# Attention over an adjacency matrix: which steps are summed through A (E - 1) g

## The chip, the cores and the metric

One core of one Trainium2 chip. The metric is the device time of one execution in microseconds (us); lower is better. The kernel before was run three times.

## The reference

Two layers on x (4096 x 512) with a 0/1 matrix adj (4096 x 4096). Layer 0 is graph attention with 8 heads of 64 features:

```python
feats = jnp.einsum('nf,hfo->hno', X, W)
dense = s_self[:, :, None] + s_neigh[:, None, :]
dense = jnp.where(dense > 0, dense, ALPHA * dense)
dense = dense * A[None, :, :]
attn = jax.nn.softmax(dense, axis=-1)
out = jnp.einsum('hij,hjo->hio', attn, feats) + b[:, None, :]
```

The result goes through relu, is added to x and normalised (layernorm). The softmax runs over all 4096 columns: a place where A is 0 has score 0 and so weight 1. Layer 1 is attention inside 32 graphs of 128 rows each, with adj added to the scores twice, again with a residual and a layernorm.

## The kernel before, in words

exp(leaky_relu(s_i + s_j)) is, up to factors of i alone and j alone, a maximum of a value of i and a value of j. So for a head and a node j, the weights against 1024 rows i are `max(p_row, d) * a`, one VectorE instruction on a 128 x 1024 tile: 128 partitions hold nodes j, the free dimension holds rows i, a is the transposed piece of the adjacency matrix. The text calls this product q.

Work is cut into passes r = 0 to 3 (a pair of heads each), chunks c = 0 to 3 (1024 rows) and steps j = 0 to 31 (128 nodes). Three sums are built in PSUM for every chunk, over its 32 steps:

- `acc` gets q times the features g_s (L1581): 8 matmul instructions a step, shown as 16 rows, each on a quarter of TensorE's columns;
- `accf` gets a times the features f_s (L1558): 4 matmuls a step, 128 x 128 weights and 512 columns;
- `dens` gets the marks times e_b (L1597), where a mark says whether q is above a bound. ScalarE makes most marks (L1544), VectorE every eighth (L1539).

At the end of a chunk `sums_to_rows` adds them up: L1278 reads accf into ys, L1286 adds acc, ScalarE copies dens (L1288), and later pieces turn ys back to rows (L1335, L1338, L1361, L1362). accf, acc and dens have one buffer each.

A *folded* step leaves its four L1558 matmuls out. VectorE makes q in two instructions for each head instead of one: L1522, `max(p_row, d) * U_row`, and L1525, `(q - c) * a`. The product of this q with g_s goes into accf (L1581, "accf<-q" in the profile), and its marks come from L1529. `folded(j)` (L1447) says which steps these are; only the first and the last pass have any. U_row is a pair of rows of the current chunk, 512 KB each, loaded by SP in `rows_for_folded` (L1453): in tiles "ck" in the first pass, "hst" and "U_row" in the last. SP, too, loads a (L635, "at"), f_s, g_s, p_row and u_row.

The first three passes go in cycles of 8 steps, the last in groups of 4. In a cycle TensorE does first all L1558, then all L1581, then dens. q has 6 buffers in the last pass and 8 in the first. In the first pass the kernel also turns the matrix: a_b pieces are loaded by POOL (L605), transposed on TensorE (L617), cast on ScalarE (L628) and written to HBM by POOL (L629) for the later passes.

In the last pass, layer 1 runs between the sums. PLANS (L1396) gives, for each group of a chunk, the pieces of the two blocks "a" and "b" that TensorE does between L1558 and L1581. Group 7 has "aaba": `rows_out` of rows 0 and 1 (L1200, read by L1202 on VectorE), `values` of 2 and 3 (L1186, read by L1194), the scores of block b (L1141, read by L1150), `rows_out` of 2 and 3. These pieces share three PSUM banks. The order on TensorE is the order of the program; the instructions of VectorE, ScalarE, POOL and SP are put in order by a scheduler when the kernel is built.

Of the kernel before, what the change touches and what calls it, by code (L numbers as in the profile page):

```python
# [404 lines left out]
def adjacency_streamed_path(  # L405
# [32 lines left out]
    NT = N // P  # L438
# [23 lines left out]
    g_d = dram.tile([PR, NT // 4, P, 4 * FP], F32, name="g_d")  # L462
    f_d = dram.tile([PR, NT // 4, P, 4 * 2 * FP], F32, name="f_d")
    FOLDED = (0, PR - 1)
    FOLDS = {4: (1,), 5: (0, 1), 6: (0, 1, 2)}, {2: (1,), 4: (1,), 5: (0, 1), 6: (0, 1, 2)}
    HU = 2 * len(FOLDED)
    pu_d = dram.tile([2 * H + HU, N], F32, name="pu_d")
    at_d = dram.tile([NCH, NT, P, C], F32, name="at_d")
# [957 lines left out]
    def main_pass(r, ae=None, wide=4):  # L1426

        for c in range(NCH):
# [18 lines left out]
            def folded(j):  # L1447

                if r == PR - 1:
                    return r in FOLDED and c > 0 and j % 4 in FOLDS[c > 1].get(j // 4, ())  # L1450
                return r in FOLDED and j % 8 == 2 and (0 if c else 8) < j < NT - 8

            def rows_for_folded():  # L1453

# [35 lines left out]
            for j0 in range(0, NT, wide):  # L1490
# [16 lines left out]
                if any(map(folded, range(NT))) and j0 == (4 if r else 0):  # L1507
                    rows_for_folded()
# [6 lines left out]
                for j in cycle:  # L1515
                    for h in range(2):
# [3 lines left out]
                        if folded(j):  # L1520
                            cn = c_all[r][:, j, h : h + 1]
                            nc.vector.scalar_tensor_tensor(  # L1522
                                q, p_row[h], d_j, U_row[h], op0=OP.max, op1=OP.mult
                            )
                            nc.vector.scalar_tensor_tensor(  # L1525
                                q, q, cn, ats[r, c, j].bitcast(F32), op0=OP.subtract, op1=OP.mult
                            )
                            mark = marks[j, h] = sgp.tile([P, C], FP8, name="mark")
                            nc.scalar.activation(  # L1529
                                mark, q, AF.Sigmoid, bias=below_0, scale=2.0**80, saturate=False  # L1530
                            )
                            continue
# [22 lines left out]
                for j in cycle:  # L1555
                    for w in range(0 if folded(j) else 2):
                        for s in range(2):
                            nc.tensor.matmul(  # L1558
                                accf[:, s, :],
                                f_s[j // 4][:, j % 4, w, :],  # L1560
                                ats[r, c, j][:, ts(s, HB)],
                                start=(j == 0 and w == 0),
                                stop=(j == NT - 1 and w == 1),
                            )
# [92 lines left out]
@with_exitstack  # L1657
def tile_gat_then_graph_attention(ctx: ExitStack, tc: tile.TileContext, *args: bass.AP):
    nc = tc.nc
    keep = ctx.enter_context(tc.tile_pool(name="flag", bufs=1))  # L1660
    flag = keep.tile([1, 1], I32, name="flag")
    adjacency_streamed_path(tc, flag, *args)
    other = nc.values_load(flag[0:1, 0:1], min_val=0, max_val=1)
    with tc.If(other > 0):
        general_path(tc, *args)
# [42 lines left out]
```

## Time and profile before

| | |
|---|---|
| median of 3 runs | 2040.63 us (2040.04 to 2043.24) |
| profiled execution | 2043.19 us, its span 2041.3 us |
| mean granted TensorE clock | 0.994 |
| TensorE busy | 2005.9 us, 98% |
| VectorE busy | 1744.8 us, 85% |
| ScalarE busy | 1533.1 us, 75% |
| POOL busy | 231.0 us |

The profile comes from one execution. PE is TensorE, DVE VectorE, ACT ScalarE, SP and POOL the engines that issue DMAs. L1558 is line 1558 of the kernel. A group's row gives the line, the engine, the operation, its output and inputs, the shapes and the count, then the busy time and the mean of one in ns, then the idle time of the engine before them and what ended it. A timeline row has the start, the time that it covers and, in brackets, the idle time before it with its releaser. Matmuls overlap at their ends, so a row's duration is a little longer than the distance to the next row's start. Setup takes the first 160 us, the first pass runs to 567, the last from about 1355 to 1920.

### The profile page before, as it was taken

How to read it: one execution, taken by the hardware profiler on the slowest of the kernel's cores; microseconds unless marked ns; L12 is line 12 of the kernel's file. 1: busy time of each engine (PE TensorE's matmuls, PEld its weight loads, DVE VectorE, ACT ScalarE, POOL GpSimd, SP SyncE). 2: the span in 40 equal slices, each digit the busy share in tenths (PEclk: the TensorE clock that was granted, in tenths of full speed). 3: DMA queues.
4: the chain of work that ended last, by engine and by line, in shares of the span. 5: the costliest groups of instructions: out<-in, count | busy, mean ns of one | idle time of the engine just before them, and what ended most of it. 6: DMA issues, size and time to landing. Idle time of an engine off the chain costs nothing.

```text
span 2041.3 us, 38200 instructions
## 1 busy us (share of the span) xinstructions
PE 2005.9 (98%) x14981; PEld 1030.0 (50%) x14981; DVE 1744.8 (85%) x2219; ACT 1533.1 (75%) x1872; POOL 231.0 (11%) x362
## 2 busy tenths in 40 slices
PE   8999999999999999999999999999999999999997
PEld 7885545444444444444444544444444444445443
DVE  5668898898999998798999989999997897889754
ACT  3348988788888889788899889999786566567420
POOL 1222222222200000000000000000020210211111
PEclk9999999999999999999999999999999999999999
DMA  6899999999999999788999999989975775775211
GB/s 206 240 320 280 283 286 288 285 280 282 316 377 342 346 359 342 261 311 292 318 321 338 313 328 338 335 277 368 323 277 186 249 255 173 232 273 176 73 55 44
DMA packets 209386, 558.70 MB, mean 274 GB/s; under 512 B 25052, under 2 KB 66012, under 8 KB 209196
## 3 DMA queue, kind: packets, MB, share of 16 engines
q1 hardware_dynamic: 144844, 433.65, 61.0%
q0 software_dynamic: 62272, 121.98, 23.3%
q8 instruction: 120, 1.97, 0.4%
q10 hardware_dynamic: 2080, 0.52, 0.1%
q14 instruction: 70, 0.57, 0.1%
HBM read 499.13 MB, written 107.28 MB: 297 GB/s over the span
## 4 chain that ended last, share of the span: by engine, by line
PE 85%; DMA 7%; DVE 5%; issue 1%; ACT 1%; SPq 0%; POOL 0%; POOLq 0%; DVEq 0%; ACTq 0%
PE acc L1581 35%; PE accf L1558 20%; PE ps_fe L818 5%; PE ps_m L1186 5%; PE ps_m L1114 5%; PE dens L1597 5%; DMA a_b<-in_adj_dram 4%; DVE q L1534 3%; PE accf L1581 2%; PE ps_m L1141 1%; PE ps_m L1200 1%; DMA hp_l<-hs_d 1%; PE ps_m L617 1%; DMA at_d<-at 1%; PE ps_m L1043 1%
## 5 line engine op out<-in xcount | busy, mean ns | idle before, releaser
L1534 DVE SCALAR_TENSOR_TENSOR q<-p_row,d_all,at 128x1024 f32<-128x1024 f32 x962 | 1168.1, 1279 | 106.0 <-PE acc L1581 78.8
L1544 ACT ACTIVATE mark<-q,nb_all 128x1024 fp8e4<-128x1024 f32 x834 | 926.8, 1144 | 174.7 <-DVE q L1534 160.1
L1581 PE MATMUL acc<-q,g_s 128*32 128x512 f32 x7696 | 853.7, 594 | 1.1 <-DVE q L1534 0.4
L1581 PEld LDWEIGHTS acc<-q,g_s 128*32 128x32 f32 x7696 | 250.2, 110 | 557.2 <-issue 496.3
L1558 PE MATMUL accf<-at,f_s 128*128 128x512 f32 x1924 | 469.3, 400 | 1.7 <-ACT at L628 1.6
L1558 PEld LDWEIGHTS accf<-at,f_s 128*128 128x128 f32 x1924 | 357.2, 189 | 107.3 <-issue 27.8
L1249 ACT ACTIVATE ck<-ck,neg_half_f 128x1024 f32<-128x1024 f32 x128 | 146.0, 1141 | 28.5 <-DMA ck<-in_adj_dram 28.4
L1250 ACT ACTIVATE ck<-ck,neg_quarter 128x1024 f32<-128x1024 f32 x128 | 146.3, 1143 | 1.8
L1597 PE MATMUL dens<-mark,e_b 128*6 128x512 fp8e4 x2048 | 125.3, 379 | 2.5 <-DVE mark L1539 2.5
L818 PE MATMUL ps_fe<-w_sb_f,xT_f 128*128 128x264 f32 (+1 forms) x512 | 121.6, 395 | 1.7 <-ACT xT_f L730 1.7
L628 ACT CAST at<-ps_m 128x1024 fp32r<-128x1024 fp8e4 x124 | 116.3, 1022 | 4.8 <-issue 2.0
L1186 PE MATMUL ps_m<-wvT,x1T 128*128 128x512 f32 x256 | 114.2, 594 | 0.0
L1114 PE MATMUL ps_m<-x1T,M_sb 128*128 128x512 f32 x256 | 113.1, 595 | 0.0
L818 PEld LDWEIGHTS ps_fe<-w_sb_f,xT_f 128*128 128x128 f32 x512 | 100.5, 200 | 16.2 <-ACT xT_f L730 2.3
L1372 POOL DMA_DIRECT2D hs_d<-hst x12 | 10.7, 896 | 828.1 <-DVE hst L1362 817.5
L1539 DVE TENSOR_SCALAR mark<-q,d_all 128x1024 fp8e4<-128x1024 f32 x128 | 96.2, 751 | 4.7
L629 POOL DMA_DIRECT2D at_d<-at x128 | 69.1, 540 | 272.5 <-ACT at L628 94.0
L1597 PEld LDWEIGHTS <-e_b 128*6 128x6 bf16 x2048 | 55.9, 86 | 80.1 <-issue 38.2
L1529 ACT ACTIVATE mark<-q,below 128x1024 fp8e4<-128x1024 f32 x62 | 69.6, 1153 | 24.5 <-DVE q L1525 24.2
L1114 PEld LDWEIGHTS ps_m<-x1T,M_sb 128*128 128x128 f32 x256 | 48.0, 190 | 58.9 <-issue 57.1
L1525 DVE SCALAR_TENSOR_TENSOR q<-q,c_all,at 128x1024 f32<-128x1024 f32 x62 | 77.3, 1273 | 0.0
L1186 PEld LDWEIGHTS ps_m<-wvT,x1T 128*128 128x128 f32 x256 | 47.7, 190 | 56.3 <-issue 55.1
(207 smaller groups left out, 1294.9 us busy)
## 6 DMA issues: line engine op xcount, KB each, us to landing
at<-at_d SPq DMA_DIRECT2D x384, 512.0 KB, 6.1
f_s<-f_d SPq DMA_DIRECT2D x128, 512.0 KB, 7.8
at_d<-at POOLq DMA_DIRECT2D x128, 512.0 KB, 19.1
ck<-in_adj_dram SPq DMA_DIRECT2D x128, 512.0 KB, 5.5
g_s<-g_d SPq DMA_DIRECT2D x128, 256.0 KB, 5.9
f_d<-fst POOLq DMA_DIRECT2D x16, 1024.0 KB, 7.5
a_b<-in_adj_dram POOLq DMA_DIRECT2D x32, 512.0 KB, 21.7
p_row<-pu_d SPq DMA_DIRECT2D x32, 512.0 KB, 6.7
```

The source lines that it names most:

```text
L628: ends_of_setup["ACT"] = nc.scalar.copy(at, both[:, :, k])
L818: nc.tensor.matmul(pf[:, q, :, cols], tile_j(xTs[k][:, c].rearrange("p u n -> p (u n)"), u), w_sb[:, c, 4 * q : 4 * q + 4, cols], start=(c ...
L1114: nc.tensor.matmul(pz, L1["M"][:, f, ts(c, P)], x1T[:, f, :], start=(f == 0), stop=(f == FC - 1),)
L1186: nc.tensor.matmul(pv, x1T[:, f, ts(u, P)], L1["wvT"][:, f, :], start=(f == 0), stop=(f == FC - 1),)
L1249: tc.keep_in_program_order(nc.scalar.activation(ck, ck, AF.Square, bias=neg_half))
L1250: nc.scalar.activation(ck, ck, AF.Abs, bias=neg_quarter, accum_out=binp[:, k : k + 1])
L1534: ends_of_setup["Q"] = nc.vector.scalar_tensor_tensor(q, p_row[h], d_j, ats[r, c, j].bitcast(F32), op0=OP.max, op1=OP.mult)
L1539: nc.vector.tensor_scalar(mark, q, d_j, None, op0=OP.is_gt, saturate=False)
L1544: nc.scalar.activation(mark, q, AF.Sigmoid, bias=nb_all[:, j, hh : hh + 1], scale=BIG, saturate=False,)
L1558: nc.tensor.matmul(accf[:, s, :], f_s[j // 4][:, j % 4, w, :], ats[r, c, j][:, ts(s, HB)], start=(j == 0 and w == 0), stop=(j == NT - 1 an ...
L1581: nc.tensor.matmul(dst[o : o + 32, s, :], g_s[j // 4][:, j % 4, h, o % FH : o % FH + 32], qs[j, h][:, ts(s, HB)], start=(j == 0), stop=(j ...
L1597: nc.tensor.matmul(dens[lo : lo + 6, :], e_b[:, j, 2 * r + h, :], marks[j, h][:, ts(s, HB)], start=(j == 0), stop=(j == NT - 1),)
```

## The change

Other steps are folded. In the first pass: before, j = 10 and 18 in chunk 0, and 2, 10 and 18 in chunks 1 to 3 (11 steps); after, 8, 16 and 24 in each chunk (12 steps). In the last pass, chunk 0 has none; the steps 28 and 29 (group 7) are added in chunks 1 and 2, chunk 3 stays as it is (20 steps before, 24 after). In all 31 steps before and 36 after.

```diff
-    FOLDS = {4: (1,), 5: (0, 1), 6: (0, 1, 2)}, {2: (1,), 4: (1,), 5: (0, 1), 6: (0, 1, 2)}
+    FOLDS = {1: {4: (1,), 5: (0, 1), 6: (0, 1, 2), 7: (0, 1)}, 2: {2: (1,), 4: (1,), 5: (0, 1), 6: (0, 1, 2), 7: (0, 1)}, 3: {2: (1,), 4: (1,), 5: (0, 1), 6: (0, 1, 2)}}
...
                 if r == PR - 1:
-                    return r in FOLDED and c > 0 and j % 4 in FOLDS[c > 1].get(j // 4, ())
-                return r in FOLDED and j % 8 == 2 and (0 if c else 8) < j < NT - 8
+                    return r in FOLDED and c > 0 and j % 4 in FOLDS[c].get(j // 4, ())
+                return r in FOLDED and j % 8 == 0 and j > 0
```

## The prediction

> **What bounds the kernel now.** I read the page first, then TensorE's waits, then the timeline of the places that the change touches.
>
> ```profile
> PE 2005.9 (98%) x14981; PEld 1030.0 (50%) x14981; DVE 1744.8 (85%) x2219; ACT 1533.1 (75%) x1872; POOL 231.0 (11%) x362
> ...
> PE   8999999999999999999999999999999999999997
> ...
> DMA  6899999999999999788999999989975775775211
> ...
> L1581 PE MATMUL acc<-q,g_s 128*32 128x512 f32 x7696 | 853.7, 594 | 1.1 <-DVE q L1534 0.4
> ...
> L1558 PE MATMUL accf<-at,f_s 128*128 128x512 f32 x1924 | 469.3, 400 | 1.7 <-ACT at L628 1.6
> ```
>
> TensorE is busy 98% of the span, so work taken off it pays where nothing else is ready to stall it. DMA is at 9 tenths through the first pass (160 to 567 us). TensorE's largest waits are few:
>
> ```profile
> PE ps_m L617 <- DMA a_b<-in_adj_dram: 6.2, 3, 3.6
> PE dens L1597 <- DVE mark L1539: 2.5, 3, 1.5
> ```
>
> Before and after fold the same number of steps ahead of those three a_b waits (3 in each preceding stretch), so they should stay. The place that matters is group 7 of the last pass's chunk 1, TensorE:
>
> ```profile
> 1566.72 5.36 PE L1581 MATMUL accf<-q,g_s 128*32 128x512 f32 x48
> 1571.90 1.90 PE L1581 MATMUL acc<-q,g_s 128*32 128x512 f32 x16
> 1573.73 3.96 PE L1558 MATMUL accf<-at,f_s 128*128 128x512 f32 x16
> 1577.53 1.88 PE L1200 MATMUL ps_m<-v_t,a 128*128 128x512 f32 x4
> 1579.24 7.03 PE L1186 MATMUL ps_m<-wvT,x1T 128*128 128x512 f32 x16
> ```
>
> and VectorE in the same stretch:
>
> ```profile
> 1568.74 3.68 DVE L1534 SCALAR_TENSOR_TENSOR q<-p_row,d_all,at 128x1024 f32<-128x1024 f32 x3 [8.14 <-PE accf L1581]
> 1572.33 0.75 DVE L1539 TENSOR_SCALAR mark<-q,d_all 128x1024 fp8e4<-128x1024 f32 x1
> 1573.00 6.06 DVE L1534 SCALAR_TENSOR_TENSOR q<-p_row,d_all,at 128x1024 f32<-128x1024 f32 x5
> 1578.98 0.74 DVE L1202 SCALAR_TENSOR_TENSOR y_f<-ps_m,rd_f,x1b 128x512 f32<-128x512 f32 x1
> ```
>
> The reader is to see that VectorE idles 8.14 us until the first accf<-q matmuls free a q buffer, then runs without a hole, and gets to L1202 only after eight sums. L1202 ends at 1579.7; TensorE's second L1186 tile, which takes the PSUM bank that it empties, starts at 1579.24 + 3.43 = 1582.7 (half of the x16 row). So there are 3.0 us of room.
>
> **What the Trainium skill says.** "PSUM — Partial Sum Buffer", Engine vs sequencer instructions: VectorE's queue is a strict FIFO. The trace agrees as far as it can: L1202 starts where the eighth sum ends, though its matmul began 1.45 us earlier. "TensorE: Matmul & The Clock Gate", Part 1: an idle window of about 3.4 us halves TensorE's clock until it has been busy as long. The trace has one such gap:
>
> ```profile
> 379.89 1.07 PE L617 MATMUL ps_m<-ident_b,a_b 128*128 128x128 bf16 x16 [3.63 <-DMA a_b<-in_adj_dram]
> 380.88 5.31 PE L1581 MATMUL acc<-q,g_s 128*32 128x512 f32 x32
> ```
>
> and, one cycle of the same kind later in the same pass,
>
> ```profile
> 426.72 6.69 PE L1558 MATMUL accf<-at,f_s 128*128 128x512 f32 x28
> ...
> 434.25 3.64 PE L1581 MATMUL acc<-q,g_s 128*32 128x512 f32 x32
> 437.71 1.90 PE L1581 MATMUL accf<-q,g_s 128*32 128x512 f32 x16
> ```
>
> After 3.63 us of idleness the 32 matmuls took 5.14 us until the next row (386.02); without it 3.46. So one such gap costs 1.7 us beyond itself. "DMA: Bandwidth & Descriptors", Issuing engines are not separate DMA queues: transfers of all queues share 16 engines. Fits the a_b waits behind loads that SP issues.
>
> **The change, part by part.**
> Removed: 4 L1558 matmuls in each of 5 more folded steps (31 to 36). 32 take 7.44 us (452.77 to 460.21), 28 take 6.53 (426.72 to 433.25): 0.91 to 0.93 a step in the first pass; 16 take 3.80 in the last, 0.95 a step. All on TensorE: 5 x 0.93 = 4.6 us if nothing else is late. L1581 work is the same, only its destination differs.
> Added: two more sums of 1.2 us per folded step on VectorE, 10 in all, 12 us.
>
> First pass. One step more, in chunk 0 (8, 16, 24 for 10, 18). In chunks 1 to 3 three steps stay three, moved from cycles 0 to 2 to cycles 1 to 3 and to the head of the cycle. VectorE's cycle is 20.5 us unfolded and 22.9 folded, plus 2.5 where L1278 and L1286 come in, against TensorE's 24.85: its waits for acc (0.75 to 1.9 us in each folded cycle) cover the sums, and those of the head step are made during the previous cycle's acc stretch, since the ring of 8 lets VectorE run four steps ahead. Without that cover one sum costs 1.2 us. L1278 moves behind the last sums of cycle 3, since accf now ends there; its reader is the next chunk's accf, more than 1 us off. SP moves the two 512 KB row loads of each chunk one cycle later, past u_row, f_s and at loads; they wait for the last L1522 and block nothing that is due within that cycle. POOL's order is the same. I take -0.9 us; the ends are -2 and +8 (three row pairs of about 2.8 us of full DMA put wholly on the a_b waits).
>
> Last pass, chunk 1, group 7 (28 and 29 fold). L1558 goes from x16 to x8: L1200 starts at 1575.7, not 1577.5. The first L1186 tile runs 1577.4 to 1580.8. The second must wait for the first L1202. In the order built for the changed kernel that L1202 stands on VectorE behind twelve sums and a mark (L1534 and L1539 of step 27, L1522 and L1525 of 28 and 29, L1534 of 30), and they can't start earlier than 1568.74 (q buffers): 1568.74 + 12 x 1.195 + 0.67 = 1583.75, and 0.65 for itself: 1584.4. TensorE stands still for 3.6 us. Then L1186 to 1587.9, L1141 (3.57) to 1591.45, L1200 (1.81) to 1593.25, where acc began at 1591.49: +1.8 instead of -1.9. Behind the L1202 also queue the second L1202, the statistics and L1194 (ends 1588.5, before L1200 needs it), the sums of step 31 (ready 1597.8, due 1598.5) and L1278, now at 1598.8 to 1600.0, due at accf's start, 1602.1.
>
> Next chunk. Before, its step 3 was late by 1.4 us, for VectorE (1610.96: 16 matmuls took 3.04 where 1.75 is usual, after 0.21 idle). After, VectorE's sums of step 3 end at about 1612.9, TensorE's group 0 at 1614.7 against 1614.0: a part of the delay is absorbed, +0.7. Then the second L1186 tile of that group takes the bank of L1215 and waits for ScalarE's L1217 (0.58 and the hand-over): +0.8, and the later sums of step 7 add about 0.4: +1.9 at the end. SP's row loads for chunk 2 now wait for the L1522 of step 29 (about 1580) and stand ahead of three at loads needed from 1602 on; a load takes 6.1 us, so 15 us of room.
>
> Chunk 2 repeats this 165.4 us later (the timeline has the same rows at 1732.13 to 1763.77). Its follower, chunk 3, has both L1362 together and no bank wait: +1.6.
>
> Sum: -0.9 + 1.9 + 1.6 = +2.6 us. On the profiled execution (2043.19, span 2041.3) that is 2045.8; the median of the runs is 2040.63, so 2043.2. The bounds of the last pass: -3.7 (stall wholly absent) and +6.9 (+1.7 of clock twice).
>
> **The rivals.** (Same means within 0.2%, 4.1 us, about what a measurement of this kernel can tell from no change.)
> *TensorE-bound throughout.* All five steps give their 0.93: 2036.0. For it: 98% busy, and a stall in one place can be paid back by an earlier one (the 1.4 us of step 3). Against: the L1202 has only 3.0 us of room, and the fold takes 1.85 + 4 x 1.195 = 6.6 from it.
> *The clock falls.* Faster and unchanged end here: if the gap in group 7 reaches the length that brought the clock down at 379.89 (3.63 us; mine is 3.6), each of the two costs 1.7 more: 2043.2 + 3.4 = 2046.6, slower. It decides at a gap of about 3.4 to 3.6 us. Against: one case in the trace; a 2.19 us gap at 487.78 shows none.
> *The rows meet the a_b loads.* The moved row loads lengthen the three waits at chunk starts by 2.8 us each: 2043.2 + 8.4 = 2051.6. For: DMA is full there. Against: the waits fall in cycle 0 of the next chunk, the loads land a cycle away.
> *The fold loses in the first pass, too.* The sums at the head of a cycle stall acc by 1.2 us in 12 cycles: at most 14.4 on top, 2057.6. Against: 0.75 to 1.9 us of VectorE idleness in each.
>
> **How the numbers follow.** Stalls as worked out, 2043.2: 0.46. Clock falls, 2046.6: 0.20. TensorE-bound or nearly, about 2036: 0.25. Rows or head sums: 0.09. Of the first case a tenth ends above 2044.7, and of the faster case a tenth above 2036.5. So faster 0.24, same 0.44, slower 0.32. The range leaves out the rival of the rows and the far half of the faster one: 2035.0 to 2049.0; the likeliest case's own is 2041 to 2045.
>
> **What would show it.** In group 7 of chunks 1 and 2: L1558 x8, then an idle of 3 to 4 us ahead of the second L1186 tile, released by L1202 on VectorE; its absence makes the prediction wrong by 3.7 a chunk. After it, a matmul row of 3.46 us that takes 5 shows the clock rival. In the first pass: cycles with 28 L1558 at 24.9 us, a_b waits of 0.4, 3.6 and 2.2 us as before; longer ones show the rows. Chunk starts of the last pass: no new idle in front of accf (L1278) or for at loads.

## The result, and the profile after

The changed kernel took 2049.45 us (median of 8 runs, 2041.63 to 2052.22), the kernel before 2040.3 us beside it (2038.0 to 2043.29). The ratio of the two is 1.0039, with a 95% interval of 1.0029 to 1.0048: slower by some 8 us. Its runs spread over 10 us, with the clock: the fastest had a mean granted TensorE clock of 0.995, the slowest, which is also the profiled execution (span 2050.4), one of 0.989. Disturbed runs are left out of the ratios, and one such run (2098.87 us) was among early4's below.

The first part of the changed kernel's page and two of its groups (busy and mean ns, then the idle time before them), and the L1186 group of the kernel before:

```profile
PE 2009.4 (98%) x14961; PEld 1025.0 (50%) x14961; DVE 1755.2 (86%) x2229; ACT 1525.7 (74%) x1872; POOL 223.7 (11%) x362
...
L1558 PE MATMUL accf<-at,f_s 128*128 128x512 f32 x1904 | 465.6, 400 | 2.4 <-ACT at L628 2.2
...
L1186 PE MATMUL ps_m<-wvT,x1T 128*128 128x512 f32 x256 | 120.5, 619 | 7.8 <-DVE y_f L1202 7.1
```

```profile
L1186 PE MATMUL ps_m<-wvT,x1T 128*128 128x512 f32 x256 | 114.2, 594 | 0.0
```

The 20 L1558 matmuls are gone (1924 to 1904), and yet TensorE is busy 3.5 us longer. L1186 has the same count as before, but its mean is 619 ns, not 594, and there is a new wait of 7.1 us ahead of it. TensorE's waits (us in total, times, longest):

```profile
PE ps_m L1186 <- DVE y_f L1202: 7.1, 2, 3.6
PE ps_m L617 <- DMA a_b<-in_adj_dram: 5.5, 2, 4.4
...
PE accf L1558 <- ACT at L628: 2.2, 4, 1.6
```

The a_b waits are about what they were in sum (6.2 us before), in two waits of 1.1 and 4.4 us where three were of 0.4, 3.6 and 2.2. The waits for ScalarE's cast (L628) were one, of 1.6 us, and are four. Group 7 of chunk 1 on TensorE's timeline:

```profile
1569.33 5.36 PE L1581 MATMUL accf<-q,g_s 128*32 128x512 f32 x48
1574.50 1.90 PE L1581 MATMUL acc<-q,g_s 128*32 128x512 f32 x16
1576.33 2.12 PE L1558 MATMUL accf<-at,f_s 128*128 128x512 f32 x8
1578.29 1.88 PE L1200 MATMUL ps_m<-v_t,a 128*128 128x512 f32 x4
1580.00 3.60 PE L1186 MATMUL ps_m<-wvT,x1T 128*128 128x512 f32 x8
1587.16 6.32 PE L1186 MATMUL ps_m<-wvT,x1T 128*128 128x512 f32 x8 [3.57 <-DVE y_f L1202]
1593.32 3.73 PE L1141 MATMUL ps_m<-x1T,zT 128*128 128x128 f32 x32
```

L1558 is down to 8 matmuls and 1.96 us. The second L1186 tile waits 3.57 us, and then takes 6.16 us to the next row where 3.43 is usual. VectorE's timeline tells why it waits:

```profile
1571.34 2.48 DVE L1534 SCALAR_TENSOR_TENSOR q<-p_row,d_all,at 128x1024 f32<-128x1024 f32 x2 [8.27 <-PE accf L1581]
...
1585.17 1.28 DVE L1534 SCALAR_TENSOR_TENSOR q<-p_row,d_all,at 128x1024 f32<-128x1024 f32 x1
1586.36 1.41 DVE L1202 SCALAR_TENSOR_TENSOR y_f<-ps_m,rd_f,x1b 128x512 f32<-128x512 f32 x2
```

L1202 starts 15.02 us after the first sum of step 27; before it was 10.24. The difference is four sums of 1.195. The granted clock (third number from the right) in just the two slow tiles of the changed kernel:

```profile
1587.16:1593.32 6.16, 6.16 (x8) 2.57 (x9) 3.55 (x8) 1.35 (x2) 2.20 (x4) 0.57 0.44 167
1757.22:1763.68 6.46, 6.46 (x8) 2.71 (x9) 3.54 (x8) 1.34 (x2) 2.17 (x4) 0.54 0.50 188
```

The columns are the stretch, its length, the busy time of TensorE, weight loads, VectorE, ScalarE and POOL, then the clock, DMA share and GB/s. TensorE ran these tiles at 0.57 and 0.54 of its clock.

From the dens row of groups 4 and 5 to that of groups 6 and 7, chunk 1 takes 60.70 us (55.79 before), chunk 2 takes 60.71 (56.02). Chunk 1's 4.9: -1.84 (L1558), +3.57 (gap), +2.73 (slower tile, that is, mainly the clock), and 0.4 of smaller shifts. In chunk 2 the slower tile costs 3.03.

### The profile page after: what moved, and what is told of

The parts are those of the page before. It is cut to its first block, busy times and chain, and to the rows that moved or that the text cites. A ratio compares the mean times of both kernels' runs of the same rounds, so it can differ in the third digit from the quotient of the medians.

```text
span 2050.4 us, 38116 instructions
## 1 busy us (share of the span) xinstructions
PE 2009.4 (98%) x14961; PEld 1025.0 (50%) x14961; DVE 1755.2 (86%) x2229; ACT 1525.7 (74%) x1872; POOL 223.7 (11%) x362
## 5 line engine op out<-in xcount | busy, mean ns | idle before, releaser
L1534 DVE SCALAR_TENSOR_TENSOR q<-p_row,d_all,at 128x1024 f32<-128x1024 f32 x952 | 1155.1, 1279 | 116.6 <-PE acc L1581 66.9
L1544 ACT ACTIVATE mark<-q,nb_all 128x1024 fp8e4<-128x1024 f32 x824 | 907.4, 1148 | 145.4 <-DVE q L1534 134.4
L1581 PE MATMUL acc<-q,g_s 128*32 128x512 f32 x7616 | 843.2, 594 | 0.6
L1581 PEld LDWEIGHTS acc<-q,g_s 128*32 128x32 f32 x7616 | 247.8, 110 | 558.5 <-issue 499.2
L1558 PE MATMUL accf<-at,f_s 128*128 128x512 f32 x1904 | 465.6, 400 | 2.4 <-ACT at L628 2.2
L1558 PEld LDWEIGHTS accf<-at,f_s 128*128 128x128 f32 x1904 | 352.2, 189 | 109.1 <-issue 26.9
L1529 ACT ACTIVATE mark<-q,below 128x1024 fp8e4<-128x1024 f32 x72 | 81.7, 1146 | 86.4 <-DVE q L1525 86.0
L1186 PE MATMUL ps_m<-wvT,x1T 128*128 128x512 f32 x256 | 120.5, 619 | 7.8 <-DVE y_f L1202 7.1
L1597 PE MATMUL dens<-mark,e_b 128*6 128x512 fp8e4 x2048 | 127.3, 379 | 0.7 <-ACT mark L1544 0.7
L628 ACT CAST at<-ps_m 128x1024 fp32r<-128x1024 fp8e4 x124 | 117.2, 1027 | 4.1 <-PE ps_m L617 4.1
L1114 PE MATMUL ps_m<-x1T,M_sb 128*128 128x512 f32 x256 | 113.1, 595 | 0.7 <-ACT x1T L1095 0.7
L1597 PEld LDWEIGHTS <-e_b 128*6 128x6 bf16 x2048 | 55.9, 86 | 77.9 <-issue 34.8
L1525 DVE SCALAR_TENSOR_TENSOR q<-q,c_all,at 128x1024 f32<-128x1024 f32 x72 | 90.7, 1277 | 0.0
L1186 PEld LDWEIGHTS ps_m<-wvT,x1T 128*128 128x128 f32 x256 | 49.4, 198 | 68.6 <-issue 58.0
L1114 PEld LDWEIGHTS ps_m<-x1T,M_sb 128*128 128x128 f32 x256 | 47.9, 190 | 60.2 <-issue 57.9
```

The costliest lines, as they stand in the source:

```text
L628: ends_of_setup["ACT"] = nc.scalar.copy(at, both[:, :, k])
L1114: nc.tensor.matmul(pz, L1["M"][:, f, ts(c, P)], x1T[:, f, :], start=(f == 0), stop=(f == FC - 1),)
L1186: nc.tensor.matmul(pv, x1T[:, f, ts(u, P)], L1["wvT"][:, f, :], start=(f == 0), stop=(f == FC - 1),)
L1534: ends_of_setup["Q"] = nc.vector.scalar_tensor_tensor(q, p_row[h], d_j, ats[r, c, j].bitcast(F32), op0=OP.max, op1=OP.mult)
L1544: nc.scalar.activation(mark, q, AF.Sigmoid, bias=nb_all[:, j, hh : hh + 1], scale=BIG, saturate=False,)
L1558: nc.tensor.matmul(accf[:, s, :], f_s[j // 4][:, j % 4, w, :], ats[r, c, j][:, ts(s, HB)], start=(j == 0 and w == 0), stop=(j == NT - 1 an ...
```

## The experiments

All were run in five rounds with the kernel before on the same chip. Each group of experiments has its own runs of before, so across groups the ratios are to be compared, not the medians. The theory: the loss is the gap ahead of L1186, made by VectorE's sums that stand ahead of L1202, and the clock that falls behind it. The rivals: the first pass's row loads; and VectorE as the bound, whatever the order.

**One part alone.** first_only has the first pass of the change and the last pass of the kernel before; last_only is the reverse.

```diff
 first_only, against the kernel before
-                return r in FOLDED and j % 8 == 2 and (0 if c else 8) < j < NT - 8
+                return r in FOLDED and j % 8 == 0 and j > 0
```

> The first pass's folds alone (8, 16, 24), the last pass as before. Theory (the loss lies in group 7 of the last pass): one step less on TensorE, -0.9 us, the three a_b waits about 0.4, 3.6 and 2.2 us as before: 2038 to 2041. Rival (the row loads meet the a_b loads): waits longer by 1 to 3 us each, 2043 or more.

> The last pass's folds alone (28 and 29 in chunks 1 and 2), the first pass as before. Theory: both gaps of 3.57 us before the second L1186 tile, and in most runs a clock drop behind them (the tile takes 6.2 us instead of 3.42): 8 to 10 us above before, with a spread of some 8 us between runs. Rival (the first pass causes the loss): no more than 1 us above before.

first_only: 2039.26 us against 2040.27, ratio 1.0001 (0.9992 to 1.0010). last_only: 2046.46, ratio 1.0033 (1.0021 to 1.0046). That is 6 to 7 us above before, where 8 to 10 were expected. The loss is the last pass's; the rival of the row loads falls. In last_only's profile both gaps are there again (3.57 and 3.56 us), and its two tiles:

```profile
1581.78:1587.01 5.23, 5.23 (x8) 2.21 (x9) 3.54 (x8) 1.35 (x2) 1.36 (x3) 0.67 0.49 183
1750.48:1755.44 4.96, 4.96 (x8) 2.22 (x9) 3.54 (x8) 1.35 (x2) 1.36 (x3) 0.71 0.50 188
```

The clock fell here too, and cost 1.8 and 1.5 us (5.23 and 4.96 less 3.43). So one such gap has cost 1.5 to 3.0 us beyond itself in four cases of four.

**A shorter gap.** In early5 and early4, some of group 7's sums are emitted after the layer-1 pieces, so that L1202 stands behind 11 and behind 9 sums. early5 asks whether the clock also falls behind a shorter gap, early4 what the folds are worth without one.

```diff
+                both = [(j, h) for j in cycle for h in range(2)]
+                late = 5 if r == PR - 1 and c in (1, 2) and j0 == NT - wide else len(both)
+                sums(both[:late])
...
                     pieces(c, j0 // 4, 0)
+                sums(both[late:])
```

(`sums` holds the loop body of L1516 to L1551; early4 has 4 for 5.)

> All folds of the change; in group 7 of chunks 1 and 2 the second q of step 30 and those of step 31 are emitted after the layer-1 pieces, so that L1202 stands behind 11 sums instead of 12. The gap should be 3.57 - 1.2 = 2.4 us. Theory [...]: second L1186 tile 3.42 us, no drop, 2039 to 2042 in all. Rival (the idle time itself is the cost, the clock goes down with any such gap): tile still over 5 us, 2046 or more.

> All folds of the change; both sums of step 30 and those of step 31 are emitted after the pieces, so that L1202 stands behind 9 sums. The gap should be under 0.3 us. Theory: the 20 L1558 matmuls are then worth their time, -4 to -6 us: 2034 to 2037. Rival (VectorE is the bound around group 7 and what is delayed comes back as waits for q or for ys): within 2 us of before.

early5: 2045.11 us, ratio 1.0027 (1.0020 to 1.0034). early4: 2040.0 us, ratio 0.9998 (0.9987 to 1.0008). Both theories hold in part. In early5's timeline and its two tiles

```profile
1580.15 3.70 PE L1186 MATMUL ps_m<-wvT,x1T 128*128 128x512 f32 x8 [2.38 <-DVE y_f L1202]
```

```profile
1580.15:1583.69 3.54, 3.54 (x9) 1.63 (x9) 3.54 (x7) 1.51 (x2) 0.91 (x1) 1.00 0.67 228
1747.29:1750.82 3.53, 3.53 (x8) 1.62 (x9) 3.53 (x7) 1.50 (x2) 0.90 (x1) 1.00 0.63 196
```

the gap is 1.19 us shorter, as expected, and the clock stays at 1.00. (The tile takes 3.54 us even so: 0.1 us of what a slow tile costs is not the clock's.) With the same folded steps, the clock fell in these profiles after 3.57 us and did not after 2.38. But this profile is of one of early5's fastest executions (2042.55 us). Five of the 21 had a mean clock of 0.991 or 0.992, as two of the 49 of before had, so that the clock may have fallen in others; no trace shows it.

The times miss what was expected: 2042 at most for early5, 2037 at most for early4. Some 3 us more go elsewhere in each. early4 has no gap in front of L1186, and in its profile the stretch of groups 6 and 7, from dens row to dens row, is 1.0 us (chunk 1) and 1.8 us (chunk 2) shorter than first_only's. But its first dens matmuls run mixed with the last of acc, which wait for VectorE:

```profile
1592.79 1.48 PE L1586 MATMUL acc<-q,g_s 128*32 128x512 f32 x10 [0.37 <-DVE q L1534]
1593.68 0.60 PE L1602 MATMUL dens<-mark,e_b 128*6 128x512 fp8e4 x4
1594.10 0.60 PE L1586 MATMUL acc<-q,g_s 128*32 128x512 f32 x2
1594.12 2.31 PE L1602 MATMUL dens<-mark,e_b 128*6 128x512 fp8e4 x28
1596.57 3.94 PE L1562 MATMUL accf<-at,f_s 128*128 128x512 f32 x16
```

(early4's L1586, L1602 and L1562 are L1581, L1597 and L1558.) Measured to the next chunk's first L1558, where all of this is over, the stretch takes 57.94 us against first_only's 57.89 in chunk 1, and 57.08 against 57.86 in chunk 2. So most of the 1.84 us that the folds save is lost within group 7 itself, at its end: from its first L1581 to that L1558, chunk 1 takes 10.35 us (1586.22 to 1596.57), first_only 8.73, and the only wait on record there is for VectorE's sums. At the next chunk's start step 3 is late as well. early4's row, and first_only's:

```profile
1601.75 8.12 PE L1586 MATMUL acc<-q,g_s 128*32 128x512 f32 x64
1609.81 2.41 PE L1186 MATMUL ps_m<-wvT,x1T 128*128 128x512 f32 x5
```

```profile
1600.80 5.36 PE L1581 MATMUL acc<-q,g_s 128*32 128x512 f32 x48
1606.36 3.11 PE L1581 MATMUL acc<-q,g_s 128*32 128x512 f32 x16 [0.21 <-DVE q L1534]
1609.40 3.70 PE L1186 MATMUL ps_m<-wvT,x1T 128*128 128x512 f32 x8
```

The 64 matmuls take 8.06 us where 7.0 is usual, but first_only, which folds nothing in group 7, takes 8.60 for the same. This row is not where the gain went.

**One step.** Step 28 alone is folded in group 7.

```diff
-    ... 7: (0, 1)}, 2: {... 7: (0, 1)}, ...
+    ... 7: (0,)}, 2: {... 7: (0,)}, ...
```

> The change with step 28 alone folded in group 7 of chunks 1 and 2 (29 as before). L1202 then stands behind 10 sums and TensorE is 0.95 us early: a gap of about 0.3 us. Theory (gap and clock were the loss): the second L1186 tile 3.42 us, and with what a backlog of 2.4 us on VectorE gives back, 2038 to 2041. Rival (a fold in group 7 costs by itself): half of the change's loss, 2044 or more.

2038.53 us, ratio 0.9996 (0.9986 to 1.0005). The gap is 0.28 us in its timeline, as worked out:

```profile
1580.90 3.70 PE L1186 MATMUL ps_m<-wvT,x1T 128*128 128x512 f32 x8 [0.28 <-DVE y_f L1202]
```

The time is as expected. So one fold in group 7 doesn't cost by itself; two of them, in this order, do.

**Less work for VectorE.** ScalarE makes all marks of chunks 1 to 3 in the last pass, in early4, in first_only, and in early4 with step 28 alone folded in group 7.

```diff
-                        if j % 4 == 3 and h == 1:
+                        if j % 4 == 3 and h == 1 and not (r == PR - 1 and c):
```

> early4, and in the last pass's chunks 1 to 3 ScalarE makes all marks, so that 8 L1539 of 0.67 us per chunk, 5.4 us, leave VectorE. Theory (what early4 gained in group 7 went back as VectorE's backlog at the next chunk's start): the slow acc rows there go back to 7.0 us, 2 to 4 us below early4, 2035 to 2038. Rival (it went back on something else, a PSUM bank or a load): as early4, 2039 to 2041.

> first_only with the same move of the marks, as the control for early4_act: group 7 is not folded. Theory: there is little backlog to relieve, 0 to 2 us below first_only, 2037 to 2039.5. Rival (the marks on VectorE are a cost everywhere in the last pass, with or without the folds): as much below first_only as early4_act is below early4.

> Step 28 alone folded in group 7, the sums of 30 and 31 emitted after the pieces, and all marks of chunks 1 to 3 on ScalarE: no gap, half of the backlog. Theory: the best of these, 2035 to 2037.5. Rival (the fold of 29 pays for itself once the gap is gone): above early4_act by 1 us or more.

early4_act: 2038.65 us, ratio 1.0000 (0.9990 to 1.0010). first_act: 2037.86, 0.999 (0.998 to 1.000). one_early4_act: 2039.63, 1.0002 (0.9993 to 1.0012). first_act's time is inside what was expected of it; early4_act's is 0.7 us above its range, and one_early4_act's 2.1 us. By the ratios, early4 gains nothing from the move (0.9998 to 1.0000) and first_only at most 0.1% (1.0001 to 0.999), with intervals that overlap. The three settle nothing. In early4_act the row of step 3 did not go back to 7.0 us, and a new wait came in:

```profile
1604.81 8.58 PE L1586 MATMUL acc<-q,g_s 128*32 128x512 f32 x64
...
1618.52 3.67 PE L1186 MATMUL ps_m<-wvT,x1T 128*128 128x512 f32 x8 [1.06 <-DVE mv_f L521]
```

With the marks gone the scheduler put VectorE's other instructions in another order, so that the experiment changed more than the one cost.

**An earlier start for VectorE.** What all of this leaves is the 8.27 us in the changed kernel for which VectorE waits before the first sum of step 27. It waits for q buffers, which group 6's q matmuls free, and those stand behind 7 us of L1114. after_ab is the changed kernel with this piece behind them; first_ab is first_only with the same move.

```diff
-    PLANS = PLAN + [("ab", ""), ("aaba", "")], PLAN + [("a", ""), ("aa", "a")]
+    PLANS = PLAN + [("a", "b"), ("aaba", "")], PLAN + [("a", ""), ("aa", "a")]
```

> The change, with one thing moved on TensorE: in group 6 of chunks 1 and 2 the piece of block b (L1114, 16 matmuls, 7 us) goes behind the group's q matmuls instead of ahead of them. The q buffers then come free 7 us earlier, so that VectorE's sums of group 7 start some 7 us earlier and its order is unchanged up to L1202. Theory (the cause is that VectorE's sums of group 7 can't start before those buffers are free, and then are late for L1202 and for the next chunk): no gap, no clock drop, nothing given back: 6 to 10 us below the change without it, and below first_only, 2032 to 2037. Rival (VectorE is short of time in the whole of the last pass, wherever its sums lie): the gap goes, but what early4 gave back is given back here too, 2038 to 2041.

> The control: first_only with the same piece moved; group 7 is not folded. Theory: the late sums of the next chunk's step 3 (1.4 us a chunk) go, 2035 to 2038, so that folding 28 and 29 on top (after_ab) is worth 2 to 4 us. Rival (the moved piece makes TensorE wait for its PSUM banks): 2040 or more.

after_ab: 2035.5 us, ratio 0.9976 (0.9968 to 0.9983). first_ab: 2040.25, 0.9997 (0.9990 to 1.0005). VectorE's order in group 7 is the changed kernel's own, up to L1202. Its timeline in after_ab:

```profile
1560.80 2.48 DVE L1534 SCALAR_TENSOR_TENSOR q<-p_row,d_all,at 128x1024 f32<-128x1024 f32 x2 [1.21 <-PE accf L1581]
...
1575.81 0.75 DVE L1202 SCALAR_TENSOR_TENSOR y_f<-ps_m,rd_f,x1b 128x512 f32<-128x512 f32 x1
```

and TensorE's:

```profile
1558.78 5.36 PE L1581 MATMUL accf<-q,g_s 128*32 128x512 f32 x48
1563.96 1.90 PE L1581 MATMUL acc<-q,g_s 128*32 128x512 f32 x16
1565.79 7.13 PE L1114 MATMUL ps_m<-x1T,M_sb 128*128 128x512 f32 x16
1572.36 2.39 PE L1558 MATMUL accf<-at,f_s 128*128 128x512 f32 x8
1574.59 1.88 PE L1200 MATMUL ps_m<-v_t,a 128*128 128x512 f32 x4
1576.30 7.03 PE L1186 MATMUL ps_m<-wvT,x1T 128*128 128x512 f32 x16
```

The idle time is 1.21 us, still 15.0 us pass from the first sum to L1202, and both L1186 tiles run as one row. The stretch of groups 6 and 7 takes 54.03 and 54.15 us (56.05 and 56.02 in first_only): the 1.9 us that two folded steps are worth. Measured to the next chunk's first L1558 it is the same gain, 55.87 and 55.99 against 57.89 and 57.86. The control shows that the move alone is worth nothing: first_ab keeps the late step 3, against what was expected of it,

```profile
1609.69 3.11 PE L1581 MATMUL acc<-q,g_s 128*32 128x512 f32 x16 [0.20 <-DVE q L1534]
```

and folding 28 and 29 on top of it is worth 4.75 us (2040.25 - 2035.5; the matmuls taken away are 3.8). after_ab's time is inside the 2032 to 2037 expected. By the ratios it is some 13 us below the change, more than the 6 to 10 expected, and the control's 2 to 4 us gain did not come. VectorE has the same sums to make in after_ab, and so the rival of VectorE as the bound, whatever the order, falls.

**How far it goes.** last_ab is after_ab with the first pass of before; after_ab3 folds step 30 too.

```diff
 after_ab3, against after_ab
-    ... 7: (0, 1)}, 2: {... 7: (0, 1)}, ...
+    ... 7: (0, 1, 2)}, 2: {... 7: (0, 1, 2)}, ...
```

> after_ab with the first pass as before (10 and 18; 2, 10 and 18). It measures what the first pass's part of the change is worth beside a last pass without the gap. Theory (its 0.93 us are about halved, since TensorE then waits for ScalarE's cast at L628): 0 to 1.5 us above after_ab, 2035 to 2037. Rival (the first pass's part costs, by its row loads): 1 us or more below after_ab.

> after_ab with step 30 folded as well (28, 29 and 30 in chunks 1 and 2): L1202 stands behind 13 sums, which with the earlier start leaves about 1 us before the second L1186 tile. Theory (with room in group 7 a fold is worth its 0.95 us): up to 2 us below after_ab, 2033.5 to 2036. Rival (what a fold adds on VectorE, 2.4 us, now comes back at the next chunk's start, as it did in early4): equal to after_ab or up to 2 us above.

last_ab: 2036.98 us beside a before of 2042.65, ratio 0.9973 (0.9963 to 0.9984). after_ab3: 2036.41, 0.9973 (0.9962 to 0.9984). Both are as fast as after_ab: the first pass's part of the change is worth nothing that can be measured, and so is a third fold (its stretches of groups 6 and 7 are 0.9 and 0.7 us shorter, and the two after chunk 2's are together 3.2 us longer). Part of that is a wait of 0.92 us at chunk 2's start and of 1.54 us at chunk 3's, for VectorE's late reading of accf:

```profile
1758.14 3.97 PE L1558 MATMUL accf<-at,f_s 128*128 128x512 f32 x16 [1.54 <-DVE ys L1278]
```

## Why the prediction was right in its mechanism and short in its size

**Direction and place: right in the gap, but the likeliest case was not the one that came.** The likeliest case was 2043.2 us, the same within 0.2%. The measured ratio on the median that the prediction used (2040.63) makes 2048.6, which is slower by that bound; the plain median, 2049.45, is 0.45 us above the range's end. The case that came is the rival of the falling clock, which had 0.20 and was set at 2046.6. That the range reaches 2048.6 is luck as far as the likeliest case goes: its own range ended at 2045.

**The gap.** "TensorE stands still for 3.6 us" in both chunks; the profile has 3.57 twice. The twelve sums from the moment the q buffers are free, 15.0 us, were measured as 15.02. Without the 5.8 us of the two slow tiles the rest fits too: from the dens row of chunk 1's groups 4 and 5 to the kernel's last dens row, the changed kernel takes 383.5 us and the kernel before 375.4, so 2.3 us are left of the 8.1, where the prediction's last pass had +3.5.

**The clock: the step that failed.** The prediction put the gap at the very point from which the rival decides (3.4 to 3.6 us) and still took the clock as steady. The Trainium skill, "TensorE: Matmul & The Clock Gate", Part 1, names an idle window of some 3.4 us. In group 7 the profiles fit that: four gaps of 3.56 and 3.57 us brought the clock to 0.54 to 0.71, two of 2.37 and 2.38 left it at 1.00. In the first pass they do not. Behind a wait of 2.23 us for a_b the clock was down (last_ab), behind one of 3.04 it was not (early5):

```profile
270.23 1.89 PE L617 MATMUL ps_m<-ident_b,a_b 128*128 128x128 bf16 x16 [2.23 <-DMA a_b<-in_adj_dram]
272.05 4.27 PE L1581 MATMUL acc<-q,g_s 128*32 128x512 f32 x32
```

```profile
379.53 1.07 PE L617 MATMUL ps_m<-ident_b,a_b 128*128 128x128 bf16 x16 [3.04 <-DMA a_b<-in_adj_dram]
380.53 13.94 PE L1586 MATMUL acc<-q,g_s 128*32 128x512 f32 x128
```

The same 16 matmuls take 1.82 us to the next row at a granted clock of 0.50, and 1.00 us at 1.00. So the runs show no sharp limit at 3.4 us, and the prediction's one case without a fall, behind 2.19 us, was no sign of safety. The price was mis-sized, too: 1.7 us, from the one case in the first pass, where the profiled execution of the change, its slowest, had 2.73 and 3.03, and that of last_only, near its median, 1.8 and 1.5. The page says that the window runs freely, which would fit the spread of 1.5 to 3.0 us and of the runs (2041.63 to 2052.22); that it is the cause of the spread was not tested.

**The next chunk's start.** Expected +0.7 us at the end of its group 0 instead of the gap's whole delay. In the changed kernel the row of 64 took 7.00 us, so the 1.4 us of step 3 were absorbed; the L1217 wait was 0.68 us (0.8 expected). That VectorE's sums are late there again where TensorE is not delayed is what early4 showed: 8.06 us, against 8.61 in the kernel before.

**The first pass: -0.9 us, nothing measured.** first_only's interval, nearly 2 us to either side, could not show 0.9 us; its trace shows where it went. The step left out a wait. With the fold at a cycle's head, TensorE reaches the later steps' L1558 0.93 us sooner, and the a tiles of these are cast just in time. first_only's timeline in chunk 3's last cycle:

```profile
554.50 3.01 PE L1558 MATMUL accf<-at,f_s 128*128 128x512 f32 x12
557.72 3.96 PE L1558 MATMUL accf<-at,f_s 128*128 128x512 f32 x16 [0.21 <-ACT at L628]
```

Those 28 matmuls take 7.1 us where 28 took 6.53 before. The third cycle of chunk 0, folded at 16 and not at 18, came out 0.40 us longer, and each chunk's fourth cycle only 0.4 to 0.5 us shorter, not 0.93. At the second pass's start the first dens row takes 2.46 us, not 1.84 (605.06 to 607.52 in the changed kernel); no wait is recorded there, and its cause is open. The a_b waits did not stay one by one, but their sum did not grow: 5.5 us in the changed kernel and 2.8 in first_only, against 6.2 before. The row loads cost nothing that shows.

**TensorE-bound throughout** (2036.0) was wrong for this kernel; its number fits after_ab (2035.5), where the last pass's folds were worth their matmuls as soon as VectorE could start in time.

What stays open: all of where the time goes back in early4, early5 and after_ab3. The traces show late sums at the end of group 7 (early4) and a late L1278 (after_ab3), but the experiment meant to take work off VectorE (early4_act) also changed its order. Open, too, is in how many executions the clock falls, since each kernel has one trace.

## What to carry to other kernels

Moving work from the busiest engine to one with spare time pays only if the second engine can start it early enough: look for what its idle time waits for, and count the instructions between that moment and the one that the first engine needs next. When such a count gives TensorE an idle time of two to four us, price a fall of the clock too, as a chance with a range and from more than one case. And when a gain vanishes, try to free the other engine earlier before giving the gain up: here one piece moved on TensorE turned a loss of 8 us into a gain of 5.

## What the runs showed of the hardware

The fall of the clock had no fixed price: 1.5, 1.8, 2.73 and 3.03 us behind gaps that agree within 0.01 us. A gap of 3.57 us on TensorE therefore cost 5.1 to 6.6 us in all; in early5's profile one of 2.38 us cost 2.5. Nor had the fall a fixed limit: behind a wait of 2.23 us (last_ab) the granted clock was 0.50 in the next row, behind one of 3.04 us (early5) it was 1.00.
